# Relu on DVE, 107 copied groups at a falling rate, and short last updates in a graph kernel

## The chip, the core and the metric

The kernel runs on one core of a Trainium2 chip. The metric is the device time of one execution in microseconds; a time is the median of several executions. A profiled execution also gives a span, from the first to the last instruction. The engines are PE (matrix products), DVE, ACT, POOL and SP; DMA engines move data between HBM and SBUF, and PE writes its results to PSUM.

## The reference

One layer of a graph network: 200000 edges, sorted by destination, on 12500 nodes with 64 features; 32 features on an edge; a hidden width of 128.

```python
msg_in = concatenate([nodes[row], nodes[col], edge_features])   # row = src, col = dst
messages = relu(msg_in @ mW1 + mb1) @ mW2 + mb2
aggregated = segment_sum(messages, col, num_segments=12500)
upd = relu(concatenate([nodes, aggregated]) @ uW1 + ub1) @ uW2 + ub2
out = layernorm(x + upd)
```

All of it is float32.

## The kernel before

**Tables.** The product of mW1 with the source node and with the destination node is computed once per node: tab_a = x @ mW1[0:64] and tab_b = x @ mW1[64:128] + mb1, both in HBM (chunk_a, chunk_b). The columns of x lie in SBUF too, spread over xtop and xbot so that for every node one of the two holds its features and the other holds zeros (zeros, L559, clears those parts with DVE memsets in steps 3 to 10).

**Steps.** The edges form 1563 tiles of 128. Six tiles are a step (SUB, 261 steps), two steps a group of twelve (SUP). In a step:

- gather (L196): POOL issues one indirect DMA per tile (L207), 128 rows of tab_a into xg, of which there are nine buffers. The first ten steps gather rows of x instead, and PE multiplies them.
- edge_part (L354): PE forms in PSUM (pc, two buffers) the part of the edge features and of tab_b, from a one-hot operand l (L365).
- node_part (L371): DVE adds xg to pc and writes h (L388, L392); ACT applies Relu to h in place (L389, L393).
- collect (L403): PE multiplies each tile of h with a one-hot matrix sel into the sums of a window of nodes (L420), then counts the edges of each node (L425).
- select (L226): DVE builds l (L233, L235) and sel (L241) for the next group, in every second step.

**Copied groups.** In a step of the list COPIED the last two tiles are not gathered. Their 128 source columns ("xc", two buffers) are built from xtop and xbot and PE multiplies them with mW1 (L368). For each column a top and a bottom one are put together: ACT adds the two columns (singly, L336) for the first ACTS = 64 columns of a group, DVE joins them with a bitwise or (joined, L343) for the other 64. The addresses are the node numbers, loaded into registers of the engine that uses them, 16 registers for up to eight columns (addresses, L311). Which columns are built in which step comes from portion (L298), at one rate for the whole run: a group every 2.5 steps, from step 16 on, 96 in all. DVE's columns of a step are dealt out in two or three parts: right behind node_part, between L235 and L241 of select, and at the end of the step.

**Updates.** UPD lists the steps at which a new period of nodes begins, 33 in all, so that the periods hold at most UN - WIN nodes; they are 47 steps apart at first and four at the end. At the end of a period close (L436) copies the sums and the counts to SBUF on ACT, update (L458) multiplies them with weights (w2u on the sums, then uz on counts and x), activated (L466) applies Relu, residual (L472) forms the output with two products per block of 128 nodes (ux, u2), then evacuate, statistics, deviation, norm and store follow in later steps. carry (L428) brings the part of the window that reaches past a period into the next one. The last period is UL = 384 columns wide.

**Order.** Every engine executes its instructions in the order in which the main loop (L750 to L807) emits them; the loop is an order written by hand. In step s it emits gathers as far ahead as buffers are known to be free, the loads of tab_b rows for step s + 2 on SP, node_part(s), the late stages of earlier updates, collect(s - 1), close, select and its loads, chunk_b up to step 50 or so, carry and update, edge_part(s + 1), residual, the columns of x for the next update on SP, the preparation of rest(s), the rest of DVE's columns, ACT's columns, activated and store.

Of the kernel before, what the change touches and what calls it, by code (L numbers as in the profile page):

```python
# [17 lines left out]
P = 128  # L18
# [54 lines left out]
FIRST, GAPS = 16, (3, 2)  # L73
COPIED = []
while FIRST + sum(GAPS) * (len(COPIED) // len(GAPS)) + sum(GAPS[:len(COPIED) % len(GAPS)]) < NSUB - 6:
    COPIED.append(FIRST + sum(GAPS) * (len(COPIED) // len(GAPS)) + sum(GAPS[:len(COPIED) % len(GAPS)]))
RNDS = -(-len(COPIED) // len(GAPS))
LAST = 4 * (N - 1)
ACTS, CHUNK = 64, 8


def updates():


    def node(s):
        return N * min(1.0, s * SUB * P / E) ** 2
    at = [0]
    for s in range(1, NSUB):
        if s > at[-1] and node(s + 1) - node(at[-1]) > UN - WIN:
            at.append(s)  # L90
    return at
# [4 lines left out]
UL = min(UB, -(-int(N * (1 - (UPD[-1] * SUB * P / E) ** 2) + WIN) // P)) * P  # L96
# [3 lines left out]
def gnn_kernel(ctx: ExitStack, tc: tile.TileContext, x1T, x, eT, e_rows, src, src_row, dst, dst_row, wlist, wrow, wnext, whalf,  # L100
# [40 lines left out]

    cols = const.tile([RNDS * len(GAPS), 2 * P], I32, name="cols")
    col_a = const.tile([RNDS * len(GAPS), P, 2], I32, name="col_a")
# [68 lines left out]
    with tc.tile_pool(name="sup", bufs=2) as sup, tc.tile_pool(name="work", bufs=2) as work, tc.manual_schedule():  # L212
# [13 lines left out]
        def select(g, at=None):  # L226
# [11 lines left out]
            if at is not None:  # L238
                joined(at, 1, 3)
# [46 lines left out]
        def columns_list():  # L286

            for r in range(len(GAPS)):
                v = src_row[:, ((FIRST + sum(GAPS[:r])) * SUB + SUB - 2) * P:]
                nc.sync.dma_start(cols[r * RNDS:(r + 1) * RNDS],  # L290
                                  bass.AP(v.tensor, v.offset, [[sum(GAPS) * SUB * P, RNDS], [1, 2 * P]]))
            cv = cols.rearrange("k (b e) -> k b e", b=2)
            for b, base in enumerate((XBASE, YBASE)):
                nc.vector.tensor_scalar(col_a[:, :, b], cv[:, b], 4.0, float(base), op0=ALU.mult, op1=ALU.add)
# [3 lines left out]
        def portion(s, total, unit):  # L298

            rate, found = sum(GAPS) / len(GAPS), []  # L300
            begin = min(c - 2 - (j + 1) * rate for j, c in enumerate(COPIED[:len(GAPS)]))
            for j, c in enumerate(COPIED):
                lo, hi = (min(-(-int(total * (s + d - begin - j * rate) / rate * 16 + 0.5) // (16 * unit)) * unit, total) for d in (0, 1))
                lo = max(lo, 0)
                if lo < hi:
                    if c not in xc:
                        xc[c] = work.tile([P, P], F32, name="xc")
                    found.append((xc[c], j % len(GAPS) * RNDS + j // len(GAPS), lo, hi))
            return found

        def addresses(k, a, m, engine):  # L311

            _, v = nc.values_load_multi_w_load_instructions(
                col_a.rearrange("k e b -> k (e b)")[k:k + 1, 2 * a:2 * m], engines=[engine], min_val=XBASE,
# [16 lines left out]
        def singly(s, part, of):  # L331

            todo = [(o, k, e) for o, k, lo, hi in portion(s, ACTS, 2) for e in range(lo, hi, 2)]
# [4 lines left out]
        def joined(s, part, of):  # L338

            todo = [(o, k, ACTS + e) for o, k, lo, hi in portion(s, P - ACTS, 2) for e in range(lo, hi, 2)]  # L340
            for o, k, a, m in share(todo, part, of):
                for e, top, bot in addresses(k, a, m, ET.DVE):
                    nc.vector.tensor_tensor(o[:, e:e + 1].bitcast(I32), top.bitcast(I32), bot.bitcast(I32),  # L343
                                            op=ALU.bitwise_or)
# [26 lines left out]
        def node_part(s):  # L371
# [12 lines left out]
            else:  # L384
                a = xg.pop(s)[0].rearrange("p (b k) f -> p b k f", b=2)
                if s in COPIED:
                    m = SUB // 2 - 1
                    nc.vector.tensor_tensor(h[:, :, :m], pc[:, :, :m], a[:, :, :m], op=ALU.add)  # L388
                    nc.scalar.activation(h[:, :, :m], h[:, :, :m], AF.Relu)  # L389
                    nc.scalar.activation(h[:, :, m:], pc[:, :, m:], AF.Relu)  # L390
                for b, m in parts(n) if s not in COPIED else []:
# [586 lines left out]
```

## Time and profile before

| | us |
|---|---|
| median of 3 runs (1739.24 to 1740.65) | 1740.07 |
| the profiled execution | 1740.13 |
| its span | 1738.4 |
| PE busy | 1451.4 (83%) |
| ACT busy | 1442.8 (83%) |
| POOL busy | 1299.3 (75%) |
| DVE busy | 1076.5 (62%) |
| mean granted clock of PE | 0.574 of full |

A line of the profile's groups names the line of the code, the engine, the operation, what is written from what, and how often; behind the bar stand the busy time, the mean length of one in ns, and the time for which the engine stood idle ahead of them with what ended the idle time. "issue" there is time in which the engine waited for nothing that the profile shows: register loads, address arithmetic and the issue of DMAs by its own sequencer. A line of the timeline has the start, the length, the engine, the line and the operation. A line of the chain that ended last has the start, the length and what ran. A line of the table of windows has the window, its length, the busy time, the granted clock of PE, the DMA share and GB/s.

### The profile page before, as it was taken

Reading aid. Unit: us, or ns where it says so; the run is one execution under the profiler, and the core shown is the slowest. Engines: PE = TensorE matmul, PEld = TensorE weight load, DVE = VectorE, ACT = ScalarE, POOL = GpSimd, SP = SyncE. Lnnn points to the kernel's source line nnn. Section 1 sums busy time; section 2 is a strip of 40 time slices with the busy share of each in tenths; the row PEclk is TensorE's granted clock in tenths of the full one; section 3 lists DMA queues with packets and bytes.
Section 4 is the critical chain, followed back from the end, with each engine's and each line's share of the span. In section 5 each row is a group of like instructions: output and inputs, shape, how many; then the busy total and the mean of one; then the engine's idle time right before and its main releaser. Section 6 shows DMA issues by size and latency. Waiting matters only on the chain. (4 is left out here: it accounts for less than half of the span.)

```text
span 1738.4 us, 46326 instructions
## 1 busy us (share of the span) xinstructions
PE 1451.4 (83%) x9598; PEld 1261.2 (73%) x9598; DVE 1076.5 (62%) x7325; ACT 1442.8 (83%) x6691; POOL 1299.3 (75%) x1380
## 2 busy tenths in 40 slices
PE   3697888888888887887988889898888888889997
PEld 2586777878777776766877777687777667777775
DVE  1566766767676656666666666666666666666642
ACT  0216998999999888988999999999999999899941
POOL 7777777777777777777777777777777777777774
PEclk8665555565555555555555555555556656565665
DMA  8773434433333333333333333333333334343342
GB/s 214 207 160 103 124 105 128 120 92 100 101 97 98 95 97 94 98 101 95 99 107 103 104 107 104 105 106 104 105 108 109 106 109 111 104 111 110 108 111 63
DMA packets 207110, 192.27 MB, mean 111 GB/s; under 512 B 57098, under 2 KB 172931, under 8 KB 206835
## 3 DMA queue, kind: packets, MB, share of 16 engines
q1 hardware_dynamic: 148418, 92.38, 19.5%
q0 software_dynamic: 43872, 87.97, 18.5%
q10 hardware_dynamic: 14546, 8.93, 1.8%
q8 instruction: 91, 1.49, 0.4%
q14 instruction: 183, 1.50, 0.3%
HBM read 171.46 MB, written 17.66 MB: 109 GB/s over the span
## 5 line engine op out<-in xcount | busy, mean ns | idle before, releaser
L207 POOL DMA_INDIRECT xg<-tab_a,src_s x1311 | 1240.8, 946 | 399.6 <-issue 361.4
L336 ACT ACTIVATE xc<-xtop,xbot 128x1 f32 x6144 | 1167.3, 280 | 41.0 <-issue 29.8
L343 DVE TENSOR_TENSOR xc<-xtop,xbot 128x1 int32 x6144 | 536.7, 154 | 410.0 <-issue 397.1
L420 PEld LDWEIGHTS sums<-sel,h 128*128 128x128 f32 x3126 | 620.3, 299 | 73.8 <-ACT h L393 27.6
L420 PE MATMUL sums<-sel,h 128*128 128x32 f32 x3126 | 643.7, 373 | 27.0 <-ACT h L393 20.2
L365 PE MATMUL pc<-rhs,l 64*128 64x128 f32 x3126 | 424.7, 418 | 183.3 <-DVE h L392 128.3
L365 PEld LDWEIGHTS pc<-rhs,l 64*128 64x128 f32 x3126 | 353.1, 297 | 248.2 <-DVE h L392 144.9
L393 ACT ACTIVATE h<-h 128x768 f32<-128x768 f32 x156 | 129.6, 831 | 128.5 <-DVE h L392 127.9
L392 DVE TENSOR_TENSOR h<-pc,xg 128x768 f32<-128x768 f32 x156 | 148.0, 949 | 128.7 <-DMA xg<-tab_a,src_s 77.9
L235 DVE TENSOR_TENSOR l<-l,cps 128x768 f32<-128x768 int32 (+1 forms) x134 | 127.8, 953 | 7.8 <-DMA l<-in_dst_row 2.5
L425 PE MATMUL cnt<-sel,one 128*1 128x32 bf16 x1563 | 84.5, 187 | 0.0
L388 DVE TENSOR_TENSOR h<-pc,xg 128x512 f32<-128x512 f32 x96 | 66.1, 689 | 22.2 <-DMA xg<-tab_a,src_s 8.7
L241 DVE TENSOR_TENSOR sel<-cps,drc 128x384 f32<-128x384 f32 x131 | 71.6, 547 | 12.0 <-PE cnt L425 11.8
L368 PE MATMUL pc<-w1a,xc 64*128 64x128 f32 x384 | 74.3, 395 | 0.0
L462 PE MATMUL pu<-sums_s,w2u 128*128 128x448 f32 (+1 forms) x66 | 61.2, 1031 | 15.5 <-DVE h L392 14.9
L207 POOL DMA_INDIRECT xg<-in_x,src_s x60 | 57.5, 958 | 19.1 <-issue 18.0
L425 PEld LDWEIGHTS <-one 128*1 128x1 bf16 x1563 | 53.9, 83 | 22.1 <-issue 8.7
L476 PE MATMUL py<-ux,xw 128*128 128x64 f32 x262 | 66.3, 344 | 1.8 <-DVE h L392 1.8
L389 ACT ACTIVATE h<-h 128x512 f32<-128x512 f32 x96 | 59.2, 617 | 9.3 <-DVE h L388 9.0
L368 PEld LDWEIGHTS pc<-w1a,xc 64*128 64x128 f32 x384 | 66.2, 308 | 0.0
L477 PE MATMUL py<-u,hTu 128*128 128x64 f32 x262 | 65.0, 340 | 0.3 <-ACT hTu L468 0.3
L476 PEld LDWEIGHTS py<-ux,xw 128*128 128x128 f32 x262 | 53.0, 250 | 7.7 <-issue 3.1
(104 smaller groups left out, 749.4 us busy)
## 6 DMA issues: line engine op xcount, KB each, us to landing
l<-in_dst_row SPq DMA_DIRECT2D x262, 96.0 KB
l<-in_eT SPq DMA_DIRECT2D x262, 96.0 KB
xg<-tab_a,src_s POOLq DMA_INDIRECT x1311
rhs<-tab_b SPq DMA_DIRECT2D x361, 32.0 KB
tab_b<-tb SPq DMA_DIRECT2D x13, 512.0 KB
rhs<-tab_b SPq DMA_DIRECT2D x387, 16.0 KB
tab_a<-tb ACTq DMA_DIRECT2D x12, 512.0 KB
out<-y SPq DMA_DIRECT2D x32, 128.0 KB
```

The costliest lines, as they stand in the source:

```text
L207: nc.gpsimd.indirect_dma_start(out=a[:, i, :] if s < XG else a[:, i // 2, i % 2, :], out_offset=None, in_=A[:, :] if s >= XG else x[:, :], ...
L235: nc.vector.tensor_tensor(l[r], l[r].bitcast(I32), node[r].unsqueeze(2).broadcast_to([r.stop - r.start, SUP // 2, P]), op=ALU.is_equal)
L241: nc.vector.tensor_tensor(s[:, :nt], slot.unsqueeze(1).broadcast_to([P, nt, WIN]), drc[:, g * SUP:g * SUP + nt].unsqueeze(2).broadcast_to( ...
L336: nc.scalar.activation(o[:, e:e + 1], top.bitcast(F32), AF.Identity, bias=bot.bitcast(F32))
L343: nc.vector.tensor_tensor(o[:, e:e + 1].bitcast(I32), top.bitcast(I32), bot.bitcast(I32), op=ALU.bitwise_or)
L365: nc.tensor.matmul(pc[:, b, k, :], L[g][q:q + 64, m, :], rhs[g % 2][q:q + 64, w, :], start=s >= XG or k == 0, stop=s >= XG and not copied)
L368: nc.tensor.matmul(pc[:, b, k, :], xc[s][q:q + 64], w1a[q:q + 64], start=False, stop=True)
L392: nc.vector.tensor_tensor(h[:, b, :m], pc[:, b, :m], a[:, b, :m], op=ALU.add)
L393: nc.scalar.activation(h[:, b, :m], h[:, b, :m], AF.Relu)
L420: nc.tensor.matmul(ps[:, bass.ds(ws[i], WIN)], h[:, i % 2, i // 2, :], S[g][:, k0 + i, :], start=False, stop=ends and i == n - 1)
L425: nc.tensor.matmul(pn[:, bass.ds(ws[i], WIN)], one, SB[g][:, k0 + i, :, 1], start=False, stop=ends and i == n - 1)
L476: nc.tensor.matmul(py[:, i], xw[u % 2][:, i * P:(i + 1) * P], ux, start=True, stop=False)
```

## The change

- **Relu.** In node_part DVE adds xg to pc in place in PSUM and then takes the maximum with 0 from PSUM into h, for whole steps in two operations and for the last, shorter step in two per half. ACT has no part in it.
- **Loads.** The columns of DVE in a step are a list (quota). fetch loads the registers of up to eight columns, join does the joins. Register loads are emitted right behind the add (eight columns, six in a copied step), right behind the Relu, and right behind L235 of select; what is left of the quota follows at the end of the step. The joins of the first two stand together behind the Relu.
- **Rate.** The number of copied groups follows progress(s): 0.47 groups a step at first, falling evenly to 0.42 at the end, from step 11 on; 107 groups, the last one in step 253. ACTS is 68 columns for ACT, DVE has 60. DVE does more of them in even steps (those with a select) and fewer in odd ones (SWING).
- **Zeros.** xtop and xbot are zeroed by ACT instead of DVE.
- **Addresses.** columns_list loads the node numbers of every step's last two tiles in two DMAs, and col_a holds them by step.
- **Order of products.** collect counts before it sums; close copies the counts before the sums; update multiplies uz before w2u; residual does all ux products before all u2 products.
- **Last updates.** The last 32 steps are cut into periods of three or four steps, so that there are 34 updates instead of 33; the last two begin at steps 256 and 259, and the last one is 192 columns wide. At step 259 the update before the last goes, through evacuate, ahead of node_part, and its statistics, norm and store follow in step 260.

```diff
-FIRST, GAPS = 16, (3, 2)
+BEGIN, FINAL = 11, 255
+RATES = 0.47, 0.42
+SWING = 0.04
+def progress(s, early=0.0):
+    s = max(s + 1 - BEGIN, 0)
+    return s * (RATES[0] + (RATES[1] - RATES[0]) * s / (2 * NSUB)) + (early if s else 0.0)
 COPIED = []
+for s in range(NSUB):
+    while min(progress(s), progress(s, -SWING if s % 2 else SWING)) >= len(COPIED) + 1 and s + 3 < FINAL:
+        COPIED.append(s + 3)
-ACTS, CHUNK = 64, 8
+ACTS, CHUNK = 68, 8
...
-    return at
+    at = [a for a in at if a < NSUB - 32]
+    steps = -(-(NSUB - 2 - at[-1]) // 4)
+    return at + [at[-1] + -(-(NSUB - 2 - at[-1]) * (i + 1) // steps) for i in range(steps)]
...
             if at is not None:
-                joined(at, 1, 3)
+                join(fetch(quota(at), CHUNK))
...
+        def quota(s):
+            if s not in quotas:
+                early = [-SWING if (s + d) % 2 else SWING for d in (-1, 0)]
+                quotas[s] = [(o, c, ACTS + e) for o, c, lo, hi in portion(s, P - ACTS, early) for e in range(lo, hi, 2)]
+            return quotas[s]
+        def fetch(todo, n):
+            ready = []
+            while todo and n:
+                o, c, a = todo[0]
+                m = min(len([t for t in todo if t[1] == c]), n // 2)
+                del todo[:m]
+                n -= 2 * m
+                ready += [(o, *x) for x in addresses(c, a, a + 2 * m, ET.DVE)]
+            return ready
+        def join(ready):
+            for o, e, top, bot in ready:
+                nc.vector.tensor_tensor(o[:, e:e + 1].bitcast(I32), top.bitcast(I32), bot.bitcast(I32),
+                                        op=ALU.bitwise_or)
...
-                if s in COPIED:
-                    m = SUB // 2 - 1
-                    nc.vector.tensor_tensor(h[:, :, :m], pc[:, :, :m], a[:, :, :m], op=ALU.add)
-                    nc.scalar.activation(h[:, :, :m], h[:, :, :m], AF.Relu)
-                    nc.scalar.activation(h[:, :, m:], pc[:, :, m:], AF.Relu)
-                for b, m in parts(n) if s not in COPIED else []:
-                    nc.vector.tensor_tensor(h[:, b, :m], pc[:, b, :m], a[:, b, :m], op=ALU.add)
-                    nc.scalar.activation(h[:, b, :m], h[:, b, :m], AF.Relu)
+                m = SUB // 2 - (s in COPIED)
+                todo = quota(s)
+                if n == SUB:
+                    nc.vector.tensor_tensor(pc[:, :, :m], pc[:, :, :m], a[:, :, :m], op=ALU.add)
+                    ready = fetch(todo, CHUNK - 2 * (s in COPIED))
+                    nc.vector.tensor_scalar(h, pc, 0.0, None, op0=ALU.max)
+                else:
+                    for b, m in parts(n):
+                        nc.vector.tensor_tensor(pc[:, b, :m], pc[:, b, :m], a[:, b, :m], op=ALU.add)
+                        nc.vector.tensor_scalar(h[:, b, :m], pc[:, b, :m], 0.0, None, op0=ALU.max)
+                    ready = []
+                join(ready + fetch(todo, CHUNK))
...
-            py = psum.tile([P, UB, D], F32, name="py", tag="pc")
+            py = psum.tile([P, UB, D], F32, name="py", tag="sums" if u + 2 == K else "pc")
             for i in range(blocks(u)):
-                nc.tensor.matmul(py[:, i], xw[u % 2][:, i * P:(i + 1) * P], ux, start=True, stop=False)
-                nc.tensor.matmul(py[:, i], hT[:, i * P:(i + 1) * P], u2, start=False, stop=True)
+                nc.tensor.matmul(py[:, i], xw[u % 2][:, i * P:(i + 1) * P], ux, start=i == 0, stop=False)
+            for i in range(blocks(u)):
+                nc.tensor.matmul(py[:, i], hT[:, i * P:(i + 1) * P], u2, start=False, stop=i + 1 == blocks(u))
...
-            nc.vector.memset(xtop[D:, i * w:(i + 1) * w], 0.0)
-            nc.vector.memset(xbot[:D, i * w:(i + 1) * w], 0.0)
+            for t in (xtop[D:], xbot[:D]):
+                nc.scalar.activation(t[:, i * w:(i + 1) * w], ident[:D, 0:1].broadcast_to([D, w]), AF.Copy, scale=0.0)
...
+            if s == UPD[K - 1]:
+                for stage in (evacuate, statistics, deviation, norm, store):
+                    stage(K - 3)
+                collect(s - 1)
+                for stage in (close, update, activated, residual, evacuate):
+                    stage(K - 2)
+            if s == UPD[K - 1] + 1:
+                for stage in (statistics, deviation, norm, store):
+                    stage(K - 2)
             if s < NSUB:
                 node_part(s)
-                joined(s, 0, 3 if j == 0 and g + 1 < NSUP else 2)
...
-            joined(s, 2 if j == 0 and g + 1 < NSUP else 1, 3 if j == 0 and g + 1 < NSUP else 2)
+            while s < NSUB and quota(s):
+                join(fetch(quota(s), CHUNK))
             singly(s, 0, 1)
```

68 lines of the change are left out of this document (29 added, 39 removed).

## The prediction

> **What bounds the kernel now.** The first view is the page's list of the costliest groups.
>
> ```profile
> L207 POOL DMA_INDIRECT xg<-tab_a,src_s x1311 | 1240.8, 946 | 399.6 <-issue 361.4
> L336 ACT ACTIVATE xc<-xtop,xbot 128x1 f32 x6144 | 1167.3, 280 | 41.0 <-issue 29.8
> L343 DVE TENSOR_TENSOR xc<-xtop,xbot 128x1 int32 x6144 | 536.7, 154 | 410.0 <-issue 397.1
> L393 ACT ACTIVATE h<-h 128x768 f32<-128x768 f32 x156 | 129.6, 831 | 128.5 <-DVE h L392 127.9
> L392 DVE TENSOR_TENSOR h<-pc,xg 128x768 f32<-128x768 f32 x156 | 148.0, 949 | 128.7 <-DMA xg<-tab_a,src_s 77.9
> ```
>
> POOL issues one gather per tile of 128 edges and waits for almost nothing but its own issue. In the timeline the first of the 1311 gathers from tab_a starts at 78.56 us and the last at 1717.66: (1717.66 - 78.56)/1310 = 1.251 us each, whatever else runs. A step is six tiles; where a step's last two tiles are "copied", their columns come from SBUF by ACT and DVE and POOL issues four. With 96 copied steps POOL needs (6 - 2/2.5) x 1.251 = 6.51 us a step.
>
> The second view is the timeline of DVE, beside that of POOL: I set the start of each step's L388/L392 against the end of its last gather's issue. I call the difference the **lag**. It is 36 us at step 10 (86.6 to 123.0), falls to 2.8 at step 78 and stays between 1.6 and 5 up to the end. A gather needs some 2 us to land, so from step 78 on POOL is the bound. From step 18 to 78 the compute engines ran free of it: (538.2 - 180.2)/60 = 5.97 us a step. That is their own pace, and the table of windows says whose: ACT is busy 194.00 of 200 us between 300 and 500.
>
> The third view is the chain that ended last: the last gather, then the tail.
>
> ```profile
> 1713.92 2.46 DMA xg<-tab_a,src_s
> ...
> 1716.50 0.97 DVE h L392
> ...
> 1721.19 2.51 PE sums L420 x12
> 1723.69 0.26 PE cnt L425 x6
> 1723.95 1.44 PE sums L420 x6
> ...
> 1726.02 1.65 PE pu L462 x2
> 1727.67 1.29 PE pu L463 x2
> ...
> 1728.99 0.59 ACT hTu L468
> ...
> 1729.62 0.69 PE py L477 x2
> ```
>
> The last two L392 start at 1720.68, the span ends at 1738.4: a tail of 17.7 us. The profiled execution took 1740.13 us around this span (1.73 more), and the median of the runs is 1740.07, so I add 1.7 to a span and nothing for the median.
>
> **Gathers.** 107 copied groups instead of 96 leave out 22 more tiles: 22 x 1.251 = **-27.5 us**, if POOL stays the bound up to its end. It then needs (6 - 0.94) x 1.251 = 6.33 us a step early (RATES 0.47 groups a step) and (6 - 0.84) x 1.251 = 6.46 late (0.42), 6.40 in the mean. So the question is whether ACT, DVE and PE, which start 36 us behind, can hold that pace.
>
> **ACT.** It loses the Relus (L393, L389, L390: 129.6 + 59.2 + 34.7 = 223.5 us) and its waits for DVE before them, 127.9 us on L393 alone. It gains 68 x 107 - 6144 = 1132 columns; 26 run in 4.91 us in the timeline, 0.189 each, so 214 us. A step: early 32 x 0.189 = 6.05 and one update (L439, L440, L468, L483, L498: 2.33 us) in 18 steps, 6.2; late 28.6 x 0.189 + 2.33/4 = 6.0. Below POOL's 6.33 and 6.46. The zeroing of xtop and xbot comes to ACT, 16 operations of 1568 elements; by the slope between its copies of 256 (0.37) and 512 (0.58) some 1.5 us each (bounds 1.3 and 2.0), two per step in steps 3 to 10, where ACT has only 1.3 us of work per step of 6.6. Hidden: 0; without that cover it would be 24 us. DVE loses 16 x 1.36 there, but PE paces these steps (busy 3.40 of each 3.40 us between 97 and 114 us), so I count nothing.
>
> **DVE.** Here everything added ends up, so I go by one stretch of its timeline, taken before the lag was gone:
>
> ```profile
> 303.99 0.96 DVE L392 TENSOR_TENSOR h<-pc,xg 128x768 f32<-128x768 f32 x1
> 305.20 0.65 DVE L343 TENSOR_TENSOR xc<-xtop,xbot 128x1 int32 x8 [0.25 <-issue]
> 305.76 0.22 DVE L233 TENSOR_SCALAR cps<-wh,pidx 128x6 f32<-128x6 int32 x1
> 306.01 0.95 DVE L235 TENSOR_TENSOR l<-l,cps 128x768 f32<-128x768 int32 x1
> 307.22 0.65 DVE L343 TENSOR_TENSOR xc<-xtop,xbot 128x1 int32 x8 [0.25 <-issue]
> 307.78 0.55 DVE L241 TENSOR_TENSOR sel<-cps,drc 128x384 f32<-128x384 f32 x1
> 308.72 0.65 DVE L343 TENSOR_TENSOR xc<-xtop,xbot 128x1 int32 x8 [0.39 <-issue]
> 309.28 0.69 DVE L388 TENSOR_TENSOR h<-pc,xg 128x512 f32<-128x512 f32 x1
> 310.51 0.65 DVE L343 TENSOR_TENSOR xc<-xtop,xbot 128x1 int32 x8 [0.54 <-issue]
> 311.75 0.51 DVE L343 TENSOR_TENSOR xc<-xtop,xbot 128x1 int32 x6 [0.60 <-issue]
> ```
>
> Ahead of eight joins stand sixteen register loads. Behind an operation of 0.96 us the joins start 1.21 us after it began, behind one of 0.69 us 1.23 us: the loads take 1.2 us from that start, and the operation hides its own length of them. Eight joins cost 0.56. The Relu itself (128x768 out of PSUM) is in no row; COPY 128x512 out of PSUM (L578, 0.689) equals the add of that size (L388, 0.689), so I take the add's 0.95 (bounds 0.55, by L612's pace of 2088 elements in 1.29, and 1.15, L588 with 1024). With loads behind it both ends up to 0.95 cost the same 1.21. That the add now writes PSUM no row shows either: -0.1 to +0.2, under the cover of the loads.
>
> Start to start, an even step: add and eight columns' loads 1.21, Relu and loads 1.21, sixteen joins 1.13, L233 0.25, L235 and loads 1.21, joins 0.56, L241 and loads 0.94, joins 0.56: 7.07. An odd one: 1.21 + 1.21 + 1.13, loads that only joins cover 0.7 to 1.0, joins 0.56: 4.95. The mean is **6.0 a step** (before, by the same rows, 5.5). Added to it: the statistics and norm of an update (2.1 us, every 18 steps early, every 4 late) and in steps 11 to 50 the bias add L588 (0.35 a step). Later steps have fewer joins (25 instead of 28). Against POOL: steps 11 to 50 6.45 to 6.33, lag +5; steps 50 to 200 6.1 to 6.39; steps 200 to 250 6.25 to 6.45. For what DVE waits on PE and ACT I add 0.15 a step (the free steps ran 2 to 3% over ACT's sum): lag -21 and -2. At step 250 it is 36 + 5 - 21 - 2 = 18 us. From there nothing is copied, POOL needs 7.5 a step, DVE some 4, PE 4.54 (118.27 to 122.81) and 9.1 per update every fourth step, 6.8 at half clock or 5.7 at the 0.60 granted at the end: nine steps give back 9 x 1.8 = 16. What is left I round up to **+5 us** (0 to 30).
>
> How fast PE catches up hangs on its clock, which stood at half through a stretch that was wholly busy:
>
> ```profile
> 107.60:111.00 3.40, 3.40 (x30) 0.50 0.81 162
> ```
>
> The Trainium skill (TensorE: Matmul & The Clock Gate, What's actually happening) says that about 3.4 us of sustained activity lift the clock from half to full. By that rule a PE that catches up would run at full clock and the +5 would be 0; by the row above, which disagrees, it may stay at half, and it would be nearer 12.
>
> **The short last updates.** On the tail's path only w2u is left (uz goes first, while ACT copies the sums), 192 columns wide instead of 384: 2.94 becomes 0.83; hTu 0.58 becomes 0.41; py has two blocks and only the u2 half late, 2.4 becomes 0.9; statistics and norm -0.4. Together -4.2. The Relu of the last three tiles joins the adds on DVE, +0.3. Update K-2 and its py go ahead of step 259's sums instead of behind; PE, which must still do them and one more opening, I price +0.3. **-3.6 us** (-6 to 0). The 34th update (9.1 us of PE) lies under the gathers: 0. At step 259 two stores (0.4 us of SP each, L515) and their stages go ahead of the sums; no rhs load is left to queue behind them on SP, and POOL has no part in it. The last store ends the span, as now.
>
> Sum: 1738.4 - 27.5 - 3.6 + 5 = 1712.3; + 1.7 = **1714 us**.
>
> **Rivals.** (1) *DVE becomes the bound, and it gets slower.* Everything hangs on its mean step: 6.0 to 6.2 counted. Each 0.1 us over some 240 steps is 24 us. It is free as long as lag 36 + 240 x (step - 6.40) stays under the 16 given back, at about 6.3; at 6.45 the whole gain is gone, and at 6.55 the lag at 250 is 72, nine buffers (58 us) are full, POOL waits, and the time is some 1709 + 56 = 1765. For it: gaps of 0.25 to 0.9 us stand behind most of L343's chunks and the margin is 0.25. Against it: in its free steps DVE kept up 5.9 with 5.5 counted. 0.18. (2) *The lag stays in part*, DVE at 6.33 to 6.43: 1722 to 1736. 0.20. (3) *It cancels*: 1736.6 to 1743.5, 0.05. (4) *The joins hold POOL up.* If POOL had to stand still for each of the 276 more joins at 0.071, that is 20 us, 1734 us; but POOL's gathers are 1.249 apart between 59.83 and 78.56, without a join, and 1.251 with 6144 of them. 0.02. The Trainium skill (SBUF — State Buffer, Who interferes with whom) has such a rule: a DVE operation with two SBUF inputs locks out a GpSimd instruction that reads SBUF. The trace doesn't show it here. That the change doesn't do what it says would be ACT held by something other than DVE's adds; its sum of 6.2 speaks against it, and it gives (2).
>
> **Chances.** The forecast, 1703 to 1722, has 0.55. Faster by over 0.2% (what a measurement of this kernel can tell from no change): 0.55 + 0.20 + 0.02 = 0.77; same 0.05; slower 0.18. The range 1703 to 1741 leaves out the slower case and what may fall below: it takes in a tail of -6 with no lag (1707, less 4 for rounding) and a lag of 30.
>
> **What would show it.** POOL's last gather near 1690 us and 1289 gathers still 1.25 apart: the first term. The lag at steps 50, 200 and 250 near 41, 20 and 18. Joins 1.2 us behind the start of add and Relu. No wait of ACT for h. A Relu of 0.95. POOL waits for DVE, or a lag that grows after step 50, would prove rival 1.

## The result and the profile after

| | before | changed |
|---|---|---|
| median, us | 1739.67 (4 runs, 1739.24 to 1740.65) | 1921.55 (4 runs, 1914.56 to 1924.53) |
| ratio | 1 | 1.1042, interval 1.1027 to 1.1058 |
| the profiled execution, its span | 1740.13, 1738.4 | 1919.96, 1918.2 |
| granted clock of PE, mean | 0.574 | 0.554 |

The changed kernel is 10.4% slower; 1714 was forecast. The groups of the changed kernel that answer to those shown of before:

```profile
L218 POOL DMA_INDIRECT xg<-tab_a,src_s x1289 | 1217.3, 944 | 548.4 <-issue 347.2
L346 ACT ACTIVATE xc<-xtop,xbot 128x1 f32 x7276 | 1366.6, 280 | 112.7 <-issue 63.5
L369 DVE TENSOR_TENSOR xc<-xtop,xbot 128x1 int32 x6420 | 522.4, 152 | 311.1 <-issue 220.1
L419 DVE TENSOR_SCALAR h<-pc 128x768 f32<-128x768 f32 x250 | 239.3, 957 | 72.9 <-DVE pc L417 64.8
L516 ACT COPY y<-py 128x256 f32<-128x256 f32 x33 | 12.3, 372 | 183.3 <-PE py L510 173.3
L508 PE MATMUL py<-ux,xw 128*128 128x64 f32 x268 | 64.0, 419 | 130.5 <-DVE h L419 130.5
```

The parts that were priced are there at their price: 1289 gathers, a Relu of 0.957 us, and joins that wait less for their loads (220.1 instead of 397.1 us). New are the waits of the last two lines. Before, the same two groups waited for almost nothing:

```profile
L483 ACT COPY y<-py 128x256 f32<-128x256 f32 x32 | 11.3, 353 | 0.1
L476 PE MATMUL py<-ux,xw 128*128 128x64 f32 x262 | 66.3, 344 | 1.8 <-DVE h L392 1.8
```

Now ACT waits 173.3 us for py in 32 of its 33 copies, and PE waits 130.5 us with the first py product for DVE's Relu. That is odd at first sight, since py = x @ ux + hT @ u2 reads nothing that this Relu writes. The table of waits adds two more, the first and the last line, that were not there (engine, line and what it waited for; us in sum, times, the longest):

```profile
POOL xg L218 <- DVE pc L417: 182.2, 93, 7.5
ACT y L516 <- PE py L510: 173.3, 32, 7.6
...
PE py L508 <- DVE h L419: 130.5, 30, 6.8
DVE xc L369 <- PE pc L396: 83.5, 24, 8.2
```

POOL, which bound the kernel before, is held up 93 times because its nine buffers are full: the lag, forecast at 41 us at step 50 and 20 at step 200, is 50.4 and 56.2, and 71 at step 248. So compute is behind. Where, is seen in DVE's steps. Steps far from an update (between steps 52 and 120) take 7.6 (even) and 4.8 us (odd), 6.2 in the mean, against 7.07, 4.95 and 6.0 forecast. But each update adds to such steps some 7.1 us (steps 52 to 120) and 6.75 (120 to 200) where I counted 2.1. The timeline around one update, that of step 123 (start, length, engine, line; in brackets the idle time before it and what ended it):

```profile
902.49 4.19 ACT L346 ACTIVATE xc<-xtop,xbot 128x1 f32 x22 [4.28 <-issue]
902.51 0.30 DVE L369 TENSOR_TENSOR xc<-xtop,xbot 128x1 int32 x3 [2.22 <-PE pc L396]
...
908.64 1.74 PE L393 MATMUL pc<-rhs,l 64*128 64x128 f32 x12 [4.40 <-DVE h L419]
...
911.11 0.97 DVE L417 TENSOR_TENSOR pc<-pc,xg 128x768 f32<-128x768 f32 x1
...
912.32 0.96 DVE L419 TENSOR_SCALAR h<-pc 128x768 f32<-128x768 f32 x1 [0.24 <-DVE pc L417]
...
913.43 1.94 PE L508 MATMUL py<-ux,xw 128*128 128x64 f32 x8 [3.05 <-DVE h L419]
...
915.16 1.92 PE L510 MATMUL py<-u,hTu 128*128 128x64 f32 x8
...
917.11 0.37 ACT L516 COPY y<-py 128x256 f32<-128x256 f32 x1 [4.36 <-PE py L510]
```

Read it from the bottom. ACT stands 4.36 us ahead of the copy of y, because py is late. py is late because its first product started at 913.43 only, right behind a Relu of DVE that ends at 913.28. That Relu is the one of the very step whose part PE formed just before (908.64 to 910.38): DVE had to get through its joins, the add and the Relu while PE had nothing it was allowed to do. At the top of the view is a second stop: DVE's columns wait 2.22 us until PE's copied products L396, which come behind the update's pu, have read a column buffer. ACT's next columns start at the same moment, after an idle time of 4.28 us that the profile puts down to "issue"; that ACT waits for the same buffer is my reading, which the table of waits has for 16 other stops of ACT (22.1 us for L396).

Both have a reason in the allocation of buffers, which the built program shows tile by tile. pc, pu and py share two PSUM buffers in turn. In the changed kernel 30 of 34 py tiles fall into the buffer that the newest pc has just filled, so py must wait until the last reader of that pc is done, and this is now DVE's Relu. Before, 21 of 33 fell into the buffer of pu, which ACT's hTu had released long ago, and 11 into the pc before the last. The columns xc have two buffers as well: before, the first columns of a group always fell one step behind the step in which PE reads the group that the buffer held (94 of 94); now they fall into the same step in 82 of 105.

### The profile page after: what moved, and what is told of

Its sections match the earlier page's. It is cut to its first block, busy times and chain, and to the rows that moved or that the text cites. A ratio compares the mean times of both kernels' runs of the same rounds, so it can differ in the third digit from the quotient of the medians.

```text
span 1918.2 us, 47785 instructions
## 1 busy us (share of the span) xinstructions
PE 1539.3 (80%) x9664; PEld 1336.0 (70%) x9664; DVE 1276.6 (67%) x7857; ACT 1477.3 (77%) x7496; POOL 1276.2 (67%) x1358
## 3 DMA queue, kind: packets, MB, share of 16 engines
q1 hardware_dynamic: 149056, 92.71, 17.7%
## 4 chain that ended last, share of the span: by engine, by line
POOL 29%; DVE 21%; issue 20%; PE 15%; DMA 9%; DVEq 3%; ACT 1%; SPq 1%; ACTq 0%; POOLq 0%
POOL xg L218 29%; DVE xc L369 8%; DMA xg<-tab_a,src_s 5%; PE sums L457 5%; DVE h L419 4%; DVE pc L417 4%; PE pc L393 3%; DVEq L323 3%; DVE l L246 2%; PE py L508 2%; PE py L510 1%; DMA tab_a<-tb 1%; DMA l<-in_eT 1%; PE pu L494 1%; DMA src_s<-in_src 1%
## 5 line engine op out<-in xcount | busy, mean ns | idle before, releaser
L218 POOL DMA_INDIRECT xg<-tab_a,src_s x1289 | 1217.3, 944 | 548.4 <-issue 347.2
L346 ACT ACTIVATE xc<-xtop,xbot 128x1 f32 x7276 | 1366.6, 280 | 112.7 <-issue 63.5
L369 DVE TENSOR_TENSOR xc<-xtop,xbot 128x1 int32 x6420 | 522.4, 152 | 311.1 <-issue 220.1
L457 PE MATMUL sums<-sel,h 128*128 128x32 f32 x3126 | 670.8, 383 | 12.8 <-DVE h L419 11.8
L457 PEld LDWEIGHTS sums<-sel,h 128*128 128x128 f32 x3126 | 636.7, 308 | 32.5 <-DVE h L419 16.5
L393 PE MATMUL pc<-rhs,l 64*128 64x128 f32 x3126 | 446.4, 427 | 175.3 <-DMA l<-in_eT 53.7
L393 PEld LDWEIGHTS pc<-rhs,l 64*128 64x128 f32 x3126 | 371.2, 303 | 239.5 <-issue 193.2
L419 DVE TENSOR_SCALAR h<-pc 128x768 f32<-128x768 f32 x250 | 239.3, 957 | 72.9 <-DVE pc L417 64.8
L417 DVE TENSOR_TENSOR pc<-pc,xg 128x768 f32<-128x768 f32 (+1 forms) x250 | 212.0, 848 | 107.6 <-PE pc L393 68.2
L508 PE MATMUL py<-ux,xw 128*128 128x64 f32 x268 | 64.0, 419 | 130.5 <-DVE h L419 130.5
L516 ACT COPY y<-py 128x256 f32<-128x256 f32 x33 | 12.3, 372 | 183.3 <-PE py L510 173.3
L454 PEld LDWEIGHTS <-one 128*1 128x1 bf16 x1563 | 57.6, 83 | 55.5 <-issue 46.4
L396 PE MATMUL pc<-w1a,xc 64*128 64x128 f32 x428 | 86.4, 405 | 0.0
L396 PEld LDWEIGHTS pc<-w1a,xc 64*128 64x128 f32 x428 | 77.2, 318 | 0.0
L510 PEld LDWEIGHTS py<-u,hTu 128*128 128x128 f32 x268 | 60.3, 329 | 0.0
L494 PE MATMUL pu<-xw,uz 128*128 128x448 f32 (+1 forms) x68 | 56.5, 931 | 0.0
```

What stands on the lines that cost most here:

```text
L218: nc.gpsimd.indirect_dma_start(out=a[:, i, :] if s < XG else a[:, i // 2, i % 2, :], out_offset=None, in_=A[:, :] if s >= XG else x[:, :], ...
L346: nc.scalar.activation(o[:, e:e + 1], top.bitcast(F32), AF.Identity, bias=bot.bitcast(F32))
L393: nc.tensor.matmul(pc[:, b, k, :], L[g][q:q + 64, m, :], rhs[g % 2][q:q + 64, w, :], start=s >= XG or k == 0, stop=s >= XG and not copied)
L396: nc.tensor.matmul(pc[:, b, k, :], xc[s][q:q + 64], w1a[q:q + 64], start=False, stop=True)
L417: nc.vector.tensor_tensor(pc[:, :, :m], pc[:, :, :m], a[:, :, :m], op=ALU.add)
L419: nc.vector.tensor_scalar(h, pc, 0.0, None, op0=ALU.max)
```

## The experiments

Three theories. **A**: py's PSUM buffer makes PE, and through it ACT, wait for a Relu on DVE at every update. **B**: two xc buffers are too few for the new order of the columns. **C** (rival 1 of the prediction as it stood): DVE simply has too much to do in each step. The first four kernels shared their runs of the kernel before (1742.45 us, 9 runs).

**py in a buffer of its own kind (e1).**

```diff
-            py = psum.tile([P, UB, D], F32, name="py", tag="sums" if u + 2 == K else "pc")
+            py = psum.tile([P, UB, D], F32, name="py", tag="sums")
```

> One line of the changed kernel is changed: every py tile is put into the two PSUM buffers of the sums instead of those that pc uses. Theory A (PSUM buffer): in the changed kernel py stands in the buffer of the pc tile that PE filled just before it, so it waits for DVE's Relu of a step that comes after; ACT then waits 173 us for py in 32 updates, with its columns queued behind. Then ACT's wait for py falls below 20 us, the steps of 10 to 15 us behind an update go, and the time falls by 130 to 180 us, to 1740 to 1790. Theory B (column buffers): DVE and ACT wait for PE to free one of the two xc buffers (105 us); this is untouched, so the time stays above 1880. Theory C (pace): DVE's Relu alone makes steps of 6.6 us; the time stays above 1850, and DVE is busy or loading throughout.

Measured: 1782.14 us (1779.52 to 1784.77, 2 runs), ratio 1.0228 (1.0192 to 1.0264).

```profile
ACT y L516 <- PE py L510: 49.5, 25, 9.8
...
POOL xg L218 <- DVE pc L417: 40.4, 41, 3.8
DVE xc L369 <- PE pc L396: 40.2, 18, 5.1
```

The wait of py for a Relu is gone from the table, and an update costs 2.5 and 2.1 us in the two stretches instead of 7.1 and 6.75. DVE's work is the same to the instruction, and steps far from an update take 6.2 us as before this edit. The time is in A's range and outside those of B and C; ACT's wait for py, 49.5 us, stays above the 20 that A allowed. The wait for a column buffer stays too.

**Three column buffers (e2).**

```diff
-                        xc[c] = work.tile([P, P], F32, name="xc")
+                        xc[c] = work.tile([P, P], F32, name="xc", bufs=3)
```

> The changed kernel with three xc buffers instead of two; py stays where it is. Theory A: the stalls at the updates stay, the time falls by less than 40 us, above 1880. Theory B: the waits of DVE and ACT for xc (105 us) go, and the time falls to 1800 to 1830. Theory C: no change, within 10 us of 1921.

Measured: 1880.2 us, ratio 1.0791 (1.0746 to 1.0836).

```profile
ACT y L516 <- PE py L510: 193.8, 33, 9.7
...
POOL xg L218 <- DVE pc L417: 147.6, 87, 5.9
PE py L508 <- DVE h L419: 130.2, 30, 6.7
```

The columns wait for L396 no more (DVE's adds do, 50.9 us instead of 17.4). Of A's two lines PE's stands as it was, and ACT's has grown by 20 us. An update costs 5.4 and 5.65 us. The fall of 41 us lies at the edge of what A said (less than 40) and far from B's 1800 to 1830.

**Both (e3).**

> Both edits: py in the buffers of the sums and three xc buffers. Theory A: as with the first edit alone, 1740 to 1790, a little better at most. Theory B: only here do both waits go; 1700 to 1740, and clearly below either edit alone. Theory C: above 1850. If the count of the prediction is right once these waits are gone, POOL is the bound and the time is 1705 to 1725.

Measured: 1741.84 us (1736.47 to 1746.65, 8 runs), ratio 0.9999 (0.9984 to 1.0014): all of the loss is gone, and none of the forecast gain has come. It is 40 us better than e1, where A had said "a little better at most", and clearly below either edit alone, as B had it, though not in B's 1700 to 1740: both waits count.

The four times make a sum. With three column buffers, moving py gives 1880.2 - 1741.84 = 138.4 us; with py moved, the third buffer gives 1782.14 - 1741.84 = 40.3. Together 178.7, and the changed kernel lies 1921.55 - 1741.84 = 179.7 above e3. So A is three quarters of the loss, B the rest, and C, as a cause of the loss, has fallen: DVE does the same operations in all four, and its steps far from an update take 6.1 to 6.2 us in all four. An update now costs 0.74 us in the mean, less than the 2.1 of its statistics, which lie beside loads and waits.

e3 also shows DVE's step as it was counted:

```profile
600.18 0.97 DVE L417 TENSOR_TENSOR pc<-pc,xg 128x768 f32<-128x768 f32 x1
601.42 0.96 DVE L419 TENSOR_SCALAR h<-pc 128x768 f32<-128x768 f32 x1 [0.27 <-DVE pc L417]
602.66 1.21 DVE L369 TENSOR_TENSOR xc<-xtop,xbot 128x1 int32 x16 [0.28 <-issue]
603.79 0.21 DVE L244 TENSOR_SCALAR cps<-wh,pidx 128x6 f32<-128x6 int32 x1
604.04 0.95 DVE L246 TENSOR_TENSOR l<-l,cps 128x768 f32<-128x768 int32 x1
605.27 0.65 DVE L369 TENSOR_TENSOR xc<-xtop,xbot 128x1 int32 x8 [0.28 <-issue]
605.84 0.55 DVE L252 TENSOR_TENSOR sel<-cps,drc 128x384 f32<-128x384 f32 x1
606.82 0.65 DVE L369 TENSOR_TENSOR xc<-xtop,xbot 128x1 int32 x8 [0.43 <-issue]
607.38 0.69 DVE L417 TENSOR_TENSOR pc<-pc,xg 128x512 f32<-128x512 f32 x1
```

From add to add 7.20 us (7.07 counted); the Relu begins 1.24 behind the add and the joins 1.24 behind the Relu (1.21 counted).

Where the 27.5 us of the gathers went, e3's own table of windows and the timeline of its end tell. The columns of a window: its length, then the busy time (and instructions) of PE, weight loads, DVE, ACT, POOL, the granted clock, the DMA share and GB/s.

```profile
1000.00:1100.00 100.00, 94.07 (x553) 81.36 (x550) 77.08 (x501) 92.17 (x481) 75.61 (x81) 0.52 0.40 106
1200.00:1300.00 100.00, 95.98 (x578) 81.77 (x577) 79.25 (x508) 93.40 (x488) 75.60 (x81) 0.55 0.40 108
...
1600.00:1700.00 100.00, 94.56 (x610) 75.96 (x607) 67.51 (x341) 58.72 (x291) 70.08 (x75) 0.64 0.41 108
```

POOL issues its last gather at 1691.7 us (near 1690 was forecast), and is not held up on the way. But compute stays behind: the lag is 41.7 at step 50, 28.5 at step 200, 27 at step 250 and still 26 at step 259. From 1000 us on PE is busy 93 to 96 of 100 us at a clock of 0.52 to 0.64, ACT 89 to 95 up to 1600. The lag says that POOL is no longer the bound; which engine is, the windows leave open up to step 250 (before, PE stood at 83 to 92 from 1000 us on). For the last nine steps they don't: between 1655 and 1717 us PE is busy 59.93 of 62 us, DVE 32.27 and ACT 8.84, so there PE sets the pace. The numbers of groups below take this up.

**The Relu back on ACT (e4).** The changed kernel with its two PSUM buffers and two xc buffers, and one part undone:

```diff
-                    nc.vector.tensor_scalar(h, pc, 0.0, None, op0=ALU.max)
+                    nc.scalar.activation(h, pc, AF.Relu)
...
-                        nc.vector.tensor_scalar(h[:, b, :m], pc[:, b, :m], 0.0, None, op0=ALU.max)
+                        nc.scalar.activation(h[:, b, :m], pc[:, b, :m], AF.Relu)
```

> The changed kernel with the Relu back on ACT (from PSUM, one operation of 768 elements), all else as changed, the 107 groups too. Here the buffers fall out so that py takes that of the pc tile before last. Theory A: the wait for py shrinks to below 60 us, but ACT now has 6.2 + 0.85 us of work a step: 245 x 7.05 + 190 = about 1900 to 1940. Theory C: DVE is relieved of 239 us, the time falls below 1850.

Measured: 1839.72 us, ratio 1.0559 (1.0528 to 1.0589).

```profile
DVE xc L369 <- issue: 503.9, 571, 2.6
...
POOL xg L218 <- DVE pc L417: 97.5, 72, 5.8
PEld sums L457 <- ACT h L419: 77.3, 49, 8.1
```

The wait of py for a Relu is gone here too: in this program py falls into the pc before the last in 32 updates. In its place PE's sums wait for ACT's Relu (77.3 us), and DVE's joins for their register loads (503.9 instead of 220.1), which have lost the Relu as their cover. The time is below 1850, as C had it, and not at A's 1900 to 1940; that figure counted 7.05 us of ACT a step, and ACT's columns and Relus took 1375.2 and 198.3 us, some 6.4 a step. It doesn't speak for C, since py's wait left together with the Relu, and e1 and e3 are faster with the Relu on DVE. Set beside e1, which has two xc buffers too and no such wait of py, the Relu on DVE is 57.6 us better, as far as two kernels that place py differently can be compared. So with these rates the Relu does belong on DVE; what came with it was the buffer.

**The Relu alone (i1).** The kernel before, with one part of the change:

```diff
-                if s in COPIED:
-                    m = SUB // 2 - 1
-                    nc.vector.tensor_tensor(h[:, :, :m], pc[:, :, :m], a[:, :, :m], op=ALU.add)
-                    nc.scalar.activation(h[:, :, :m], h[:, :, :m], AF.Relu)
-                    nc.scalar.activation(h[:, :, m:], pc[:, :, m:], AF.Relu)
...
+                m = SUB // 2 - (s in COPIED)
+                if n == SUB:
+                    nc.vector.tensor_tensor(pc[:, :, :m], pc[:, :, :m], a[:, :, :m], op=ALU.add)
+                    nc.vector.tensor_scalar(h, pc, 0.0, None, op0=ALU.max)
```

> The kernel before with the Relu on DVE, all else as it was. Theory A (py's buffer, 28 of 33 py in the newest pc's): on a chip where the kernel before takes 1740, 1780 to 1880 us, with 80 us or more of py's waits for DVE's h. Theory B: 1735 to 1760. Theory C: 1760 to 1790 without those waits.

Measured: 1934.41 us (1931.87 to 1936.95, 2 runs), beside 1738.31 (7 runs) of the kernel before: ratio 1.1126 (1.1103 to 1.1148).

```profile
ACT y L483 <- PE py L477: 282.1, 32, 11.6
POOL xg L207 <- DVE pc L388: 165.6, 92, 5.4
...
PE py L476 <- DVE h L389: 131.4, 27, 6.4
ACT sums_s L439 <- PE sums L420: 111.1, 33, 10.8
```

This one part costs 196 us, more than the whole change; the other parts together win some of it back. A's signs are all there, with the columns dealt out as before and ACT's wait for L368, B's sign, at 11.2 us. The time lies above the 1880 that A allowed, and above B's and C's ranges. ACT waits at each update for py and for the last sums before it, 8.8 and 3.4 us in the mean, where the changed kernel waits 5.4 for py. C has a part in it as well: steps far from an update take 6.8 (even) and 6.2 us (odd) here, 6.5 in the mean against 5.8 in the kernel before, in the same steps 52 to 120. That is POOL's own 6.51, so the lag of the start is never worked off; I estimate this part at some 30 us, the lag of i1 at step 10 (31.6 us) less the 1.6 that the kernel before has left at step 259, and the updates at the rest. How much of it is the order of the products in an update, which the change alters, was not separated.

**Fewer groups, with both waits gone (i2, i3).** e3 with other rates, on the chip of i1 and beside the same 1738.31 of the kernel before (e3 itself stands beside 1742.45, so the ratios compare the three rather than the times):

```diff
-RATES = 0.47, 0.42
+RATES = 0.455, 0.41
```

> py in the buffers of the sums, three xc buffers, 104 groups instead of 107. On a chip where the kernel before takes 1740: 1718 to 1732 if DVE sets the end, 1735 to 1740 if PE does, 1749 if POOL does.

> The same with rates of 0.44 falling to 0.40: 101 groups. POOL's last gather then comes 6 x 2 x 1.251 = 15 us later than with 107, near 1706, and with the 12 us of tail and 5 of lag nothing under 1723 is left. On a chip where the kernel before takes 1740: 1723 to 1728 if DVE or ACT sets the end with 107 groups, 1733 to 1738 if PE does.

| copied groups | time, us | ratio | lag at step 10 | 50 | 120 | 200 | 250 | 259 |
|---|---|---|---|---|---|---|---|---|
| 107 (e3) | 1741.84 | 0.9999 (0.9984 to 1.0014) | 29.7 | 41.7 | 35.5 | 28.5 | 27 | 26 |
| 104 (i2) | 1719.2 | 0.9889 (0.9872 to 0.9905) | 35.6 | 40.5 | 22.4 | 7.5 | 3.7 | 3.3 |
| 101 (i3) | 1729.46 | 0.9945 (0.9928 to 0.9962) | 34.2 | 31.7 | 3.4 | 2.6 | 6.2 | 6.2 |

Here the end is explained. With 101 groups the lag is gone at step 120 and POOL sets the time from there; with 104 it is gone at step 250, just in time, and POOL's last gather is issued at 1696 us; with 107 compute never catches up. From 104 to 107 POOL has 3 x 2 x 1.251 = 7.5 us less to do and the lag at the end is 23 us longer: compute takes at least 15 us more, 5 a group. From 104 to 101 the time grows by 10.3, of which 7.5 are POOL's six gathers. The time of i2 lies in the range for DVE as the engine that sets the end; that of i3 lies between the range for DVE or ACT (1723 to 1728) and the one for PE (1733 to 1738), so it decides nothing between them. 104 groups with both buffers is 1.1% faster than the kernel before and, by the ratios, 10.4% faster than the changed kernel: it is the version to keep, and all of its gain hangs on two buffers and three groups.

**Runs that tell nothing of time.** The kernels of i1 (labels e5, f1, g1) and i2 (e7, f3, g2, h1) had been run earlier, and so had two more: the changed kernel with three xc buffers and pu, not py, in the buffers of the sums (e6, f2), and e3 with 104 groups at a nearly even rate, 0.44 falling to 0.43 (e8, f4).

On the first of four chips:

> The kernel before with one part of the change alone: the Relu on DVE from PSUM behind the add; loads, 96 groups and updates as before. In the built program 28 of its 33 py tiles now stand in the buffer that the pc tile just before them filled (21 of 33 stood in that of pu before). Theory A (PSUM buffer): the Relu's move alone brings the stalls at the updates: ACT waits 100 us or more for py, and the time is 1840 to 1900, though there are only 96 groups. Theory B (column buffers): without the denser groups DVE's columns wait for no buffer, so the time stays at 1740 to 1780. Theory C (pace): by the rows of DVE its step becomes 5.5 + 1.2 = 6.7 us instead of POOL's 6.5, without stalls at the updates: 1770 to 1800.

> The changed kernel with three xc buffers as in the second run, and pu instead of py in the buffers of the sums. Py stays among the buffers of pc but now falls, in 32 of 34 updates, into that of the pc tile before last, whose Relu is a step earlier. Theory A: it is the one buffer and not the space that costs, so the time is close to that with py in the buffers of the sums and three xc buffers, 1735 to 1765, and ACT waits under 70 us for py. If instead it were py's sharing of pc's two buffers at all, the time would be near the 1880 us of three xc buffers alone. Theory C: no other time than 1880.

> Both edits (py in the buffers of the sums, three xc buffers) and RATES 0.455 and 0.41: 104 groups instead of 107. With both edits POOL's last gather was issued at 1691 us but DVE came 26 us behind it. Theory: compute sets the end there; three groups fewer cost POOL 3 x 2.5 = 7.5 us and save DVE some 3 x 6.8 = 20 us, so the end moves forward, 1718 to 1732. If POOL were the bound all the same, the time would rise by 7 us to 1749.

> Both edits and RATES 0.44 and 0.43: 104 groups, too, but fewer early, where DVE also has the bias adds, and more late. If only the sum of DVE's work counts, the same time as with 0.455 and 0.41, 1718 to 1732; if the lag has to be worked off before the late updates, whose products fill PE, it is slower by 5 to 15 us.

On the second, the third and the fourth:

> The kernel before with one edit: DVE, not ACT, applies the Relu, from PSUM into h, for whole steps in one add and one maximum; everything else (96 groups, loads, updates, one column rate) is as before. By the order of the PSUM buffers in the built program, this edit alone moves 28 of 33 py tiles into the buffer that the next step's pc has just filled (21 of 33 stand in the buffer of pu before it). Theory A (the buffer of py): ACT's y copies wait for py for 100 us or more in sum, and the time is 1840 to 1900 us. Theory B (two xc column buffers): the columns are dealt out as before, so no long waits for a free column buffer: 1740 to 1780. Theory C (DVE's own pace): DVE's step grows by the Relu, 0.95 us on 240 steps less the loads that it hides, and the time is 1770 to 1800 with no wait of ACT for py.

> The changed kernel with three xc buffers, and with pu, not py, in the PSUM buffers of the sums. By the order of the buffers py then takes the pc before last in 32 of 34 updates, whose Relu lies a step further back. Theory A as I state it (py waits because its buffer is that of the newest pc): ACT's y copies wait under 70 us for py and the time is 1735 to 1765 us. If py in the tag of pc is harmful wherever it stands, or pu in a buffer of the sums has to wait as much for ACT's copies, the time stays near the 1880 of three xc buffers alone.

> The changed kernel with py in the buffers of the sums and three xc buffers (1741.84 with 107 groups), and with rates of 0.455 falling to 0.41 instead of 0.47 falling to 0.42: 104 copied groups. If DVE, ACT and PE set the end (the last gather was issued 44 us ahead of it with 107 groups), 3 groups less take some 7 us each from DVE and the time is 1718 to 1732, with POOL's last gather near 1699. If POOL set it, the time would be 3 x 2 x 1.251 = 7.5 us longer, 1749.

> The same two buffers and 104 groups too, but at a nearly even rate, 0.44 falling to 0.43: fewer early, more late. If the compute engines set the end throughout, the sum of the work is that of the falling rate and the time is the same within 5 us. If it matters where the groups lie, because updates are four steps apart at the end and PE is full there, it is 5 to 15 us longer than with the falling rate.

> The kernel before with one edit: DVE, not ACT, applies the Relu, from PSUM into h, for whole steps in one add and one maximum; all else (96 groups, loads, updates, column rate) is as before. By the order of the PSUM buffers, this edit alone moves 28 of 33 py tiles into the buffer that the next step's pc has just filled (before, 21 of 33 stand in the buffer of pu). Theory A (the buffer of py): the ux products wait 80 us or more in sum for DVE's h, ACT's copies of y 100 us or more for py, and the time is 1780 to 1880 us. Theory B (two xc buffers): the columns are dealt out as before, so 1735 to 1760. Theory C (DVE's own pace): DVE's step grows by 0.95 us less the loads that it hides, and the time is 1760 to 1790 with no wait of ACT for py.

> The changed kernel with py in the buffers of the sums, three xc buffers, and rates of 0.455 falling to 0.41 instead of 0.47 to 0.42: 104 copied groups. With 107 groups (1741.84) the last gather was issued 44 us ahead of the end. If DVE, ACT and PE set the end, 3 groups less take some 7 us each from DVE and 0.85 from PE: 1718 to 1732 where DVE is the one, 1735 to 1740 where PE is. If POOL set it, 7.5 us more: 1749.

> The changed kernel with py in the buffers of the sums, three xc buffers, and rates of 0.455 falling to 0.41: 104 copied groups instead of 107 (1741.84). If DVE sets the end once the waits are gone, 3 groups less take some 7 us each from it: 1718 to 1732. If PE does, 0.85 us each: 1735 to 1740. If POOL did, 7.5 us more: 1749.

There the kernel before itself took 2493.17, 2504.48, 2501.25 and 2506.9 us, 43 to 44% more than beside all other runs; the second of these chips later ran i1 to i3 beside 1738.31. The ratios there were 0.9913, 0.9875 and 0.9881 for the Relu alone, 1.0306, 1.0159, 1.021 and 1.0219 for the 104 groups, 1.0202 and 1.0225 for pu, 1.0211 and 1.0184 for the even rate. They are even in the wrong order: the Relu alone is 11.3% slower and the 104 groups are 1.1% faster where the kernel before takes 1738 us, and here it is the Relu alone that is the faster of the two. None of the times that were expected could be compared. The timeline of f3 shows that another limit holds:

```profile
1196.08 0.16 DVE L369 TENSOR_TENSOR xc<-xtop,xbot 128x1 int32 x1 [1.24 <-issue]
1196.10 0.21 PE L457 MATMUL sums<-sel,h 128*128 128x32 f32 x1 [1.79 <-issue]
...
1196.80 0.16 DVE L369 TENSOR_TENSOR xc<-xtop,xbot 128x1 int32 x1 [0.56 <-issue]
1196.82 0.29 PEld L457 LDWEIGHTS sums<-sel,h 128*128 128x128 f32 x1 [1.83 <-issue]
...
1198.20 0.23 DVE L244 TENSOR_SCALAR cps<-wh,pidx 128x6 f32<-128x6 int32 x1 [1.24 <-issue]
```

Single instructions come 0.7 us or a multiple of it apart, on DVE and PE at once, where e3 runs sixteen joins in 1.21 us; each is as long as ever. POOL's gathers, where they wait for nobody, still follow one another after 1.25 us. What causes it no trace here shows. So the even rate stays untried at the usual pace. Of f2 one thing can be read, since it asks what PE waits for and not how long:

```profile
L508 PE MATMUL py<-ux,xw 128*128 128x64 f32 x268 | 64.0, 414 | 23.6 <-issue 13.2
```

In its program py still shares pc's buffers, but has the pc before the last in 32 updates, and of the 23.6 us only 9.8 are a wait for DVE's Relu; the Relu alone, run beside it (f1), waited 112.8 us for it. For this wait it is the newest pc's buffer, not the sharing, that matters; e4 agrees, where py also has the pc before the last and does not wait (0.0 us). What f2's placing of py is worth in time was not measured at the usual pace.

## Why the prediction was wrong

**Gathers, -27.5: right, and worth nothing.** 1289 gathers, in e3 (1221.0 + 393.1)/1289 = 1.252 us apart, the last one at 1691.7 us ("near 1690"); i2 and i3 pay for each gather at that price. The sentence held its condition: "if POOL stays the bound up to its end". It did not.

**ACT: the sum right, the queue missed.** ACT lost its wait for h and does its 7276 columns; the zeros took 16 x 1.51 us (1.5 forecast) and the lag at step 10 is 35.6, 36.4 before, so they are hidden. But ACT waits at another place, the copy of y, 173.3 us.

**DVE's step: right in free steps.** 6.2 for 6.0, Relu 0.957 for 0.95, the Relu 1.24 us behind the add and the joins 1.24 behind the Relu for 1.21.

**The step that failed: "Added to it: the statistics and norm of an update (2.1 us, every 18 steps early, every 4 late)", with 0.15 a step "for what DVE waits on PE and ACT".** I counted an update as the work that it gives to DVE and took from the kernel before that its py and its columns wait for nobody. Both were properties of the old order. An update costs 7.1 and 6.75 us in the changed kernel; e1, e2 and e3 split this into py's buffer (138.4 us of time) and the xc buffers (40.3), and i1 shows that the Relu alone is enough for py's wait. I had listed "no ACT wait for h" as a sign to look for and never asked who else waits for pc's last reader, which the change moves from ACT to DVE, an engine with joins queued ahead of it.

**The second failure, seen only in e3: "From there nothing is copied, POOL needs 7.5 a step", with PE at 5.7 and "nine steps give back 9 x 1.8 = 16".** Two of the nine steps are copied, 251 and 253, so POOL needs 6.96 us a step there: 5 us of the 16 were never to be had. The other 10 went because a step took 6.83 us and not 5.7, with PE busy 59.93 of 62 us. That is near the 6.8 of the same sentence for half the clock, but the granted clock was 0.57 in these 62 us: either PE had more to do than the sum counted, or its work did not shorten with the clock as the sum took it to. No run tells which. Of the 16 us one came back. The lag at step 250 was 27 instead of 18. At step 50 it was 41.7 for a forecast of 41, which is partly luck: it began at 29.7 in this run instead of 36 and grew by 12 instead of 5. From step 50 to 200 it fell by 13 instead of 21, so the 0.15 us a step for waits were too few by some 0.05. At step 259 the lag is 26, some 24 us more than the 2 that I had left, and e3's span of 1734.7 is 22.4 above the 1712.3 of my sum. With 104 groups the lag falls from 40.5 to 7.5 between steps 50 and 200, and the time is 1719.2. i2 speaks for work that DVE and ACT share as the cause up to step 250 (some 5 us of compute a group, of which PE has 0.8: L396 takes 86.4 us for 107 groups), but PE is as busy there, and no run takes work from one of them alone, so which of them it is stays open.

**The clock.** The forecast stood between 0 and 12 us on it. In e3 PE was busy 94.07 of the 100 us from 1000 to 1100 at a granted clock of 0.52 and 5.00 of the 5 us from 1210 to 1215 at 0.50, and in the changed kernel and e3 alike the mean stayed at 0.55 to 0.57. The Trainium skill (TensorE: Matmul & The Clock Gate, What's actually happening) lets a stretch of some 3.4 us of sustained activity lift the clock to full. These windows do not agree with it; a clock near half, the worse end, was the better guess.

**The tail, -3.6: right.** From the start of the last adds to the end of the span it was 17.7 us (1720.68 to 1738.4), and is 12.9 in the changed kernel (1905.30 to 1918.2) and 12.0 in e3 (1722.71 to 1734.7): -4.8 and -5.7, within the -6 to 0 given and 1 to 2 us more than forecast.

**The rivals.** Rival 1 had the outcome (a lag past 58 us, full buffers, POOL waiting for DVE; 182.2 us of it) with 0.18 and 1765 us, 157 us too few; its mechanism, a mean step of 6.45 or more through load gaps, was not the one. Rival 4, joins that hold POOL up, is out: e3 has 276 more joins and a pitch of 1.252 for 1.251.

## What to carry to other kernels

When an operation moves to another engine, list every tile that shares its input's buffers, and ask of each who was the last reader before and who is now; a tile that reads none of the moved data can end up waiting for it. In a rotating set of buffers, whether it does hangs on the order of allocation, which the built program shows before anything runs; give tiles that come only now and then (here py) a set of their own. And work shifted off the engine that binds has an optimum: the lag, step by step, shows on which side of it one is (gone early: shift more; never gone: shift less), and here three groups of 107 were the difference between no gain and 1.1%.

## What the runs showed of the hardware

- Sixteen register loads on DVE behind an operation out of PSUM are hidden as behind one from SBUF: joins begin 1.24 us after the start of the Relu in e3, where the kernel before had 1.21 behind its add. Without that Relu on DVE the same joins waited 503.9 us for issue instead of 220.1 (e4).
- Between the add that writes PSUM in place and the Relu that reads it DVE stands idle for 0.26 us a step in e3, which the profile names "<- DVE pc L417" (65.0 us, 224 times). It is not a wait for the add: in i1, where no register loads stand between the two, the Relu follows the add after 0.03 us (606.98 + 0.97, then 607.98), and the idle time ahead of all 250 Relus is 8.5 us. In e3 up to sixteen loads stand there, and the Relu starts 1.24 us behind the add, as the joins do behind their loads.
